# Second layer: small VectorE work and four inputs between product and sum, and the last image's output in one piece

## The chip, the cores and the metric

The kernel runs on one core of a Trainium2 chip. The metric is the device time of one execution in microseconds (us). Five engines work side by side, each through its own queue: PE (TensorE, matmuls), DVE (VectorE), ACT (ScalarE), POOL (GpSimd) and SP (SyncE, which here only issues DMA transfers). All data are 32-bit floats.

## The reference

Sixteen images of 128 channels and 56x56 pixels go through two layers. The first is a block of windowed attention with a two-layer perceptron; the change doesn't touch it. The second, cut to what matters:

```python
y = conv3x3(x, conv_w) + conv_b
seq = y.reshape(B * H * W, 8, 16)            # 8 tokens of 16 channels
xi, z = split(seq @ in_proj)
xc = silu(causal_conv(xi) + conv1d_b)
dt, Bm, Cm = split(xc @ x_proj)
dt = softplus(dt * dt_proj_w + dt_proj_b)
dA, dBx = exp(dt * A), dt * Bm * xc
for l in range(8):
    h = dA[l] * h + dBx[l]                   # 32 x 16 state values of each sequence
    ym[l] = sum(h * Cm[l]) + D * xc[l]
out = (ym * silu(z)) @ out_proj
return x + silu(group_norm(out) * gn_w + gn_b)
```

The recurrence over the eight tokens, `h = a*h + b`, is the heart of it: a product with the decay and a sum with the input.

## The kernel before

`layer0` runs first and leaves its result in DRAM, one tensor `x1[b]` of 128 x 3136 for each image. `layer1` reads it and does the second layer. It begins at about 3200 us of the span.

**Groups and steps.** An image is cut into seven groups of 448 sequences, so there are 112 groups. The outer loop runs over groups (`i`), the inner over 14 steps (`k`, 0 to 13). A state tile `h` of one token has 128 partitions (16 states and 8 of the 32 inner channels) by four quarters of 448 columns. One step handles one token and one half of the quarters (`jp`), 128x896 elements. The loop is software-pipelined: in step `k` the state of step `k` is advanced, while the decays are prepared two steps ahead, the inputs are taken in four steps ahead and spread on PE five steps ahead. Ahead of group `i`'s own steps, pieces for groups `i+1`, `i+2` and of the past groups are done by `work(i, k)`, which returns three lists, for PE and ACT, for DVE and for POOL.

**What stands in a step**, in the order in which it is issued before:

- `advance`: on DVE the product `a = a*h(l-1)` (line 947, in PSUM) and at once the sum `h(l) = a + h(l)` (948), which reads it. Steps 12 and 13 are the last token, which has no input: only a product (945), straight into `h`.
- `inject` (937, DVE): the input of a later token, `h = x*bb`. `x` is one PSUM buffer that PE fills, and `bb` is a row broadcast from DRAM.
- `decay` (919, PE): the exponents of the step two ahead, into one of two PSUM buffers `a`.
- `spread` (930, PE): fills `x` for the input of the next step, so it must wait until `inject` has read `x`.
- `decay_exp` (922, ACT): the exponential of `a`, in place.
- `weigh` (952, POOL, odd steps): `cst = h*cb`, 128x1792.
- the lists of `work`, DVE's first, then PE's, then POOL's.

The order of each engine's queue is that of the program, fixed by `_chain`.

**What `work` adds to DVE.** Step 0: `direct_mul` (906), twice 128x448, on a PSUM result that `direct` (901, PE) makes in step 13 of the group before. Steps 3 and 12: `collect` (974), 128x448. Steps 9 and 10 after a group with an odd number, and step 9 after the last group of an image: `statistics` (1022, with one 1024 for each image). So in four groups of seven there is at least one statistic.

**What `work` adds elsewhere, so far as it matters here.** PE: in step 12 `inner` for the group two ahead (838, 839), in step 13 `direct`, `skip` (967) and a `gather` (961), in step 0 two gathers, in step 1 a gather and `rate` (851), in step 3 `gate` (877), in step 4 `inner` again, in steps 5 and 6 `project_out` (995), in steps 5 to 9 the convolution of the next image (788), in step 11 `sequences` (830). ACT: `rate_log` (862, 863) in steps 5 and 7. POOL: `rate_sum` (868 to 871) in steps 6 and 8, `product` (897) in step 10.

**Buffers.** `h` and `cst` have four buffers, `x` one, `a` two. An input takes the `h` buffer of four tokens before, when `weigh` has read it: the input issued in step 12 takes that of the `weigh` of step 9.

**The end of an image.** Statistics, `group_mean`, `deviation`, `group_var` and `affine` run one to three groups later. Then `normalise` (1062, ACT) applies Silu in eight pieces of 392 columns, each between a load of the Silu table and one of the table for exponentials, `residual` (1053 to 1058) loads the image's `x1` in two halves into a single buffer `res`, and `store` (1067 on POOL, 1070 to 1072 on SP) adds and writes the whole image at the end. For the last image these groups hold nothing else: the loop runs seven groups beyond the last.

Of the kernel before, what the change touches and what calls it, by code (L numbers as in the profile page):

```python
# [10 lines left out]
F32 = mybir.dt.float32  # L11
U32 = mybir.dt.uint32
AF = mybir.ActivationFunctionType
# [4 lines left out]
P = 128  # L18
H = W = 56
HW = H * W  # L20
# [4 lines left out]
NBLK = HW // BLK  # L25
# [119 lines left out]
def _act_set(tc, name):  # L145
    tc.keep_in_program_order(tc.nc.scalar.preload_act_table_set(name))  # L146
# [566 lines left out]
def layer1(ctx: ExitStack, tc: tile.TileContext, x1, t, out):  # L713
# [99 lines left out]
    def own(jp):  # L813
        return slice(2 * jp, 2 * jp + 2)
# [124 lines left out]
    def advance(p, l, jp):  # L939

        a, before = p["a", l, jp], p["h", l - 1][:, own(jp), :]
        if l == 7:
            if jp == 0:
                p["h", l] = w4.tile([P, 4, BLK], F32, tag="h", name=f"h_{p['n']}_{l}")
            nc.vector.tensor_mul(p["h", l][:, own(jp), :], a, before)
        else:
            nc.vector.tensor_mul(a, a, before)  # L947
            nc.vector.tensor_add(p["h", l][:, own(jp), :], a, p["h", l][:, own(jp), :])  # L948

    def weigh(p, l):  # L950
        c = p["c", l] = w4.tile([P, 4, BLK], F32, tag="cst", name=f"cst_{p['n']}_{l}")
# [95 lines left out]
        nc.gpsimd.tensor_sub(gst[:, 5:6], gn_b, gst[:, 5:6])  # L1047

    half = HW // 2

    def residual(b, k):
        res = norms[b, k] = w1.tile([P, half], F32, tag="res", name=f"res_{b}_{k}")
        nc.sync.dma_start(res[0:64], x1[b][0:64, k * half : (k + 1) * half])
        if k == 0:
            nc.sync.dma_start(res[64:P], x1[b][64:P, 64 : half + 64])
        else:
            nc.sync.dma_start(res[64:P, 0 : half - 64], x1[b][64:P, half + 64 : HW])
            nc.sync.dma_start(res[64:P, half - 64 : half], x1[b][64:P, 0:64])
# [5 lines left out]
    def store(b, k, q):  # L1064
        part = slice(q * half // 2, (q + 1) * half // 2)
        xr = xrs[b][:, k * half : (k + 1) * half][:, part]
        nc.gpsimd.tensor_add(xr, xr, norms[b, k][:, part])
        if k == q == 1:
            xr = xrs[b]
            nc.sync.dma_start(outv[b, 0], xr[0:64])  # L1070
            nc.sync.dma_start(outv[b, 1, :, 64:HW], xr[64:P, 0 : HW - 64])
            nc.sync.dma_start(outv[b, 1, :, 0:64], xr[64:P, HW - 64 : HW])

    def work(i, k):


        def at(n):
            return groups[n] if 0 <= n < len(groups) else None  # L1080

        p, nxt, far, prev = at(i), at(i + 1), at(i + 2), at(i - 1)
        pe, dve, pool = [], [], []

        if prev:
            if k == 0:
                pe += [partial(gather, prev, 5), partial(gather, prev, 6)]
            if k == 1:
                pe.append(partial(gather, prev, 7))
            if k == 3:  # L1090
                dve.append(partial(collect, prev, 1))
            if k == 4:
                pool.append(partial(gated, prev, 1))
            if k in (5, 6):
                pe.append(partial(project_out, prev, k - 5))
            b = prev["b"]
            if prev["g"] % 2 and k in (9, 10):
                dve.append(partial(statistics, b, prev["g"] - 10 + k))
            if prev["g"] == NBLK - 1:
                if k == 9:  # L1100
                    dve.append(partial(statistics, b, NBLK - 1))
                if k == 12:
                    residual(b, 0)
        two = at(i - 2)
        if two and two["g"] == NBLK - 1:
            b = two["b"]
            if k == 3:
                pool.append(partial(deviation, b))
        three = at(i - 3)
        if three and three["g"] == NBLK - 1:  # L1110
            if k == 1:
                pe.insert(0, partial(group_var, three["b"], 0))
            if k == 2:
                pool.append(partial(affine, three["b"]))

        eighth = []
        for n in range(3, 7):
            past = at(i - n)
            if past and past["g"] == NBLK - 1 and k in (4, 12):
                eighth.append(partial(normalise, past["b"], 2 * (n - 3) + k // 12))  # L1120
        for n in range(4, 8):
            past = at(i - n)
            if past and past["g"] == NBLK - 1 and k == 2:
                pool.append(partial(store, past["b"], (n - 4) // 2, n % 2))
                if n == 5:
                    pool.append(partial(residual, past["b"], 1))

        if p:
            if k == 0:
                dve.append(partial(direct_mul, p))  # L1130
            if k == 7:
                pe.append(partial(skip, p, 0))
            if k in (8, 9, 10):
                pe.append(partial(gather, p, k - 7))
            if k == 12:
                dve.append(partial(collect, p, 0))
            if k == 13:
                if nxt:
                    pe.append(partial(direct, nxt))
                pe += [partial(skip, p, 1), partial(gather, p, 4)]  # L1140
                pool.append(partial(gated, p, 0))
            if k in (2, 6):
                bring(p, 0, {2: (4, 5), 6: (6,)}[k])
            if k in (1, 5, 9):
                bring(p, 1, {1: (3, 4), 5: (5, 6), 9: (7,)}[k])

        if nxt:
            if k in (1, 2):
                pe.append(partial(rate, nxt, k - 1))
            if k in (2, 6):  # L1150
                pe.append(partial(rate_exp, nxt, k // 4))
            if k in (5, 7):
                pe.append(partial(rate_log, nxt, k // 2 - 2))
            if k in (6, 8):
                pool.append(partial(rate_sum, nxt, k // 2 - 3))
            if k == 3:
                pe += [partial(gate, nxt, 0), partial(gate, nxt, 1)]
            if k == 4:
                eighth.insert(0, partial(inner, nxt, "zs", wz, w2, 0.0))
            if k == 7:  # L1160
                bring(nxt, 0, (0, 1))
            if k == 8:
                bring(nxt, 1, (1, 2))
            if k == 11:
                bring(nxt, 0, (2, 3))
            if k == 10:
                pool.append(partial(product, nxt))
            if k == 13 and not p:
                pe.append(partial(direct, nxt))

        if p and k in (5, 6, 7, 8, 9) and p["b"] + 1 < NB:
            taps = {5: (0, 1), 6: (2, 3), 7: (4,), 8: (5, 6), 9: (7, 8)}[k]
            pe.append(partial(convolve, p["b"] + 1, p["g"], taps))
        if p and p["g"] == NBLK - 1 and k == 11 and p["b"] + 2 < NB:
            load_image(p["b"] + 2)
        if two and two["g"] == NBLK - 1 and k == 2:
            pe.append(partial(group_mean, two["b"], 0))
        if far:
            if k == 11:
                pe.append(partial(sequences, far))  # L1180
            if k == 12:
                eighth.insert(0, partial(inner, far, "xc", wx, w3, c1_b))
        if eighth:
            pe = eighth + [partial(_act_set, tc, EXP_LN)] + pe
        return pe, dve, pool

    def state_step(i, k):

        i, k = i + k // 14, k % 14
        return (groups[i], 1 + k // 2, k % 2) if i < len(groups) else None  # L1190

    def input_step(i, k):
        i, k = i + k // 14, k % 14
        return (groups[i], k // 2, k % 2) if i < len(groups) else None
# [4 lines left out]
        convolve(0, i, range(9))  # L1199
    if NB > 1:  # L1200
        load_image(1)
    for i in range(-2, len(groups) + 7):
        for k in range(14):
            now = 0 <= i < len(groups)
            if now:
                advance(*state_step(i, k))
            inputs = input_step(i, k + 4) if now or (i == -1 and k >= 10) else None
            if inputs:
                inject(*inputs)
            decays = state_step(i, k + 2) if now or (i == -1 and k >= 12) else None  # L1210
            if decays:
                decay(*decays)
            inputs = input_step(i, k + 5) if now or (i == -1 and k >= 9) else None
            if inputs:
                spread(*inputs)
            if decays:
                decay_exp(*decays)
            if now and k % 2:
                weigh(groups[i], 1 + k // 2)
            pe, dve, pool = work(i, k)  # L1220
            for part in (dve, pe, pool):
                for step in part:
                    step()
    _chain(tc, start)


# [34 lines left out]
```

## Time and profile before

| | |
|---|---|
| device time, median of three runs | 8380.8 us (8372.44 to 8384.7) |
| profiled execution: span, and its own time | 8384.7 us, 8386.68 us |
| PE busy in the span | 7889.6 us, 94% |
| DVE | 7747.0 us, 92% |
| POOL | 7036.3 us, 84% |
| ACT | 5662.9 us, 68% |
| DMA of the main queue, share of 16 engines | 34.7% |
| mean granted TensorE clock | 0.983 |

The span runs from the first to the last instruction of one profiled execution. Busy time of PE is modelled at the end of each matmul. In the chain of work that ended last, DVE holds 40% of the span, POOL 24%, PE 18%, ACT 7%, and 11% is time in which an engine waited for nothing that the profile shows. The second layer's three DVE groups of 128x896, lines 937, 947 and 948, hold 11%, 10% and 6% of it by line.

The end of the span: the last product of the recurrence starts at 8333.14 us, the last statistics at 8344.24, the first Silu of the last image at 8348.72, the last output is issued from 8374.55 to 8378.4, and the span ends at 8384.7.

### The profile page before, as it was taken

The numbers are of one execution on the slowest core, as the hardware profiler recorded it, in microseconds if no ns is written. First come the engines' busy times: TensorE is split into PE (matmuls) and PEld (weight loads), VectorE is DVE, ScalarE is ACT, GpSimd is POOL, SyncE is SP. The second block draws the span as 40 slices with busy tenths as digits, with TensorE's granted clock in tenths as the row PEclk, the third lists the DMA queues.
The fourth block names the chain that finished last, engine by engine and source line by source line (L and its number), as shares of the span: only waits on it lengthen the run. The fifth ranks groups of instructions, "written<-read, shape, count | busy, mean of one in ns | idle before, by whom it ended". The sixth has DMA issues, their size and how long they took to land.

```text
span 8384.7 us, 151590 instructions
## 1 busy us (share of the span) xinstructions
PE 7889.6 (94%) x52860; PEld 3323.8 (40%) x52860; DVE 7747.0 (92%) x10358; ACT 5662.9 (68%) x10598; POOL 7036.3 (84%) x5664
## 2 busy tenths in 40 slices
PE   6999999999999987999999999999999999999997
PEld 2444444444444443333333333333333333333332
DVE  7999999999999874999999999999999999999997
ACT  4777767777777654666666666666666666666665
POOL 5888888888887724899999999999999989999987
PEclk8999999999999998999999999999999999999998
DMA  2333333333333222334334334334334333343333
GB/s 60 86 86 87 86 89 87 87 87 87 87 88 88 75 74 70 85 92 105 92 94 107 86 96 108 83 103 108 83 103 103 87 101 102 88 104 102 88 90 81
DMA packets 764424, 757.86 MB, mean 90 GB/s; under 512 B 188688, under 2 KB 663952, under 8 KB 761616
## 3 DMA queue, kind: packets, MB, share of 16 engines
q1 hardware_dynamic: 763664, 748.18, 34.7%
q8 instruction: 422, 6.91, 0.4%
q14 instruction: 338, 2.77, 0.1%
HBM read 439.61 MB, written 102.76 MB: 65 GB/s over the span
## 4 chain that ended last, share of the span: by engine, by line
DVE 40%; POOL 24%; PE 18%; issue 11%; ACT 7%; DMA 1%; SPq 0%; POOLq 0%; ACTq 0%; DVEq 0%
DVE h L937 11%; DVE a L947 10%; DVE h L948 6%; POOL cst L952 5%; POOL xh L264 4%; POOL e L380 4%; DVE lepe L461 4%; PE a L919 4%; POOL tap L262 3%; PE x L930 2%; POOL dtx L871 2%; PE pq L788 2%; DVE sst L364 2%; PE pq L961 2%; DVE ud L906 2%
## 5 line engine op out<-in xcount | busy, mean ns | idle before, releaser
L952 POOL TENSOR_TENSOR cst<-h,cb 128x1792 f32<-128x1792 f32 x784 | 3129.4, 3998 | 374.8 <-DVE h L948 301.2
L922 ACT ACTIVATE a<-a 128x896 f32<-128x896 f32 x1568 | 1416.4, 903 | 1119.0 <-PE x L930 681.5
L937 DVE TENSOR_TENSOR h<-x,bb 128x896 f32<-128x896 f32 x1568 | 1697.7, 1083 | 164.0 <-PE x L930 123.7
L461 DVE SCALAR_TENSOR_TENSOR lepe<-vpad,lep,lepe 128x448 f32<-128x448 f32 x2688 | 1718.7, 679 | 0.6
L930 PE MATMUL x<-dtx,amask 32*128 32x448 f32 x6272 | 1618.5, 592 | 32.5 <-DVE h L937 24.9
L919 PE MATMUL a<-dt,adec 32*128 32x448 f32 x6272 | 1615.6, 591 | 35.4 <-DVE h L948 15.9
L948 DVE TENSOR_TENSOR h<-a,h 128x896 f32<-128x896 f32 x1344 | 1467.0, 1092 | 45.8
L947 DVE TENSOR_TENSOR a<-a,h 128x896 f32<-128x896 f32 x1344 | 1465.5, 1090 | 6.0 <-ACT a L922 6.0
L380 POOL TENSOR_SCALAR e<-e,sst,zero 128x256 f32<-128x256 f32 x1568 | 861.3, 559 | 454.9 <-DVE sst L376 390.7
L370 ACT ACTIVATE e<-ps,sst 128x256 f32<-128x256 f32 x1568 | 729.6, 470 | 543.0 <-DVE sst L364 488.1
L788 PE MATMUL pq<-x1pad,conv 128*128 128x448 f32 x2016 | 886.5, 559 | 27.5 <-DMA x1pad<-x 19.2
L919 PEld LDWEIGHTS a<-dt,adec 32*128 32x128 f32 x6272 | 472.4, 184 | 1050.7 <-DVE h L948 469.1
L264 POOL TENSOR_TENSOR xh<-xh,tap 128x448 f32<-128x448 f32 x735 | 841.8, 1145 | 42.6
L961 PE MATMUL pq<-cst,sel 128*32 128x448 f32 x6272 | 730.4, 551 | 1.0 <-POOL cst L952 1.0
L146 ACT ACT_TABLE_LOAD x491 | 630.0, 1283 | 9.5 <-PEq L1252 0.7
L402 PE MATMUL ptt<-ident,e 128*128 128x128 f32 x3136 | 545.6, 285 | 92.3 <-POOL e L380 74.5
L930 PEld LDWEIGHTS x<-dtx,amask 32*128 32x128 f32 x6272 | 473.3, 184 | 398.8 <-DVE h L937 378.2
L364 DVE TENSOR_REDUCE sst<-ps 128x2 f32<-128x512 f32 x784 | 540.6, 690 | 88.7 <-PE ps L358 67.1
L358 PE MATMUL ps<-sel,q 32*64 32x256 f32 x6272 | 540.2, 413 | 70.9 <-ACT e L370 64.0
L262 POOL TENSOR_SCALAR tap<-xpad,pos,zero 128x448 f32<-128x448 f32 x735 | 532.3, 724 | 34.4
L402 PEld LDWEIGHTS ptt<-ident,e 128*128 128x128 f32 x3136 | 367.0, 142 | 417.7 <-POOL e L380 240.7
L788 PEld LDWEIGHTS pq<-x1pad,conv 128*128 128x128 f32 x2016 | 348.6, 190 | 412.9 <-issue 392.6
(163 smaller groups left out, 12116.2 us busy)
## 6 DMA issues: line engine op xcount, KB each, us to landing
sel<-kv SPq DMA_DIRECT2D x3136, 64.0 KB
bb<-db SPq DMA_DIRECT2D x336, 448.0 KB
cb<-dc SPq DMA_DIRECT2D x336, 448.0 KB
xpad<-x SPq DMA_DIRECT2D x32, 784.0 KB
x<-r SPq DMA_DIRECT2D x112, 224.0 KB
x1pad<-x SPq DMA_DIRECT2D x16, 1568.0 KB
db<-bs SPq DMA_DIRECT2D x112, 224.0 KB
dc<-cs SPq DMA_DIRECT2D x112, 224.0 KB
```

Source lines behind the costliest of these rows:

```text
L264: nc.gpsimd.tensor_add(im["xh"][i], im["xh"][i], held["tap"])
L380: nc.gpsimd.tensor_scalar(e, e, im["st", w][:, 2, p : p + 1], zero, ALU.mult, ALU.add)
L402: nc.tensor.transpose(ptt[:, P * (2 * p + h) : P * (2 * p + h + 1)], e[:, h * P : (h + 1) * P], ident)
L461: nc.vector.scalar_tensor_tensor(out, src, lep[:, k : k + 1], acc, ALU.mult, ALU.add)
L788: nc.tensor.matmul(pc, lhsT=conv[:, k, :], rhs=pad[:, 8 * i + dy : 8 * i + dy + 8, dx : dx + W], start=(k == 0), stop=(k == 8),)
L919: nc.tensor.matmul(a[:, k, :], lhsT=adec[rows, l4, :], rhs=p["dt"][rows, h, :], start=True, stop=True)
L922: nc.scalar.activation(p["a", l, jp], p["a", l, jp], AF.Exp)
L930: nc.tensor.matmul(x[:, k, :], lhsT=mask[rows, l4, :], rhs=p["dtx"][rows, h, :], start=True, stop=True)
L937: nc.vector.tensor_mul(p["h", l][:, own(jp), :], px["x"], weight)
L947: nc.vector.tensor_mul(a, a, before)
L948: nc.vector.tensor_add(p["h", l][:, own(jp), :], a, p["h", l][:, own(jp), :])
L952: nc.gpsimd.tensor_mul(c, p["h", l], p["gate", 1, l].unsqueeze(1).to_broadcast([P, 4, BLK]))
```

## The change

Three things are changed, all in `layer1`.

1. `advance` keeps the product alone; the sum moves to a new function `complete`. Between the two the loop now runs DVE's list from `work` (`direct_mul`, `collect`, `statistics`).
2. In steps 2, 7, 10 and 11 (`BETWEEN`), where that list is empty, `inject` stands between product and sum instead, and `spread` for the next step is issued ahead of `decay` on PE. In the other steps the order is product, list, sum, input.
3. For the last image `finish` takes the place of `normalise` and `store`: one load of the Silu table, then four times Silu on ACT and an add on DVE, and the output in two halves. Its two residual halves are loaded in steps 4 and 6 of the last group, the second into a buffer of its own (that of an image's `xr`). The loop ends four groups earlier.

```diff
@@ advance
             nc.vector.tensor_mul(p["h", l][:, own(jp), :], a, before)
         else:
             nc.vector.tensor_mul(a, a, before)
-            nc.vector.tensor_add(p["h", l][:, own(jp), :], a, p["h", l][:, own(jp), :])
+
+    def complete(p, l, jp):
+        if l < 7:
+            h = p["h", l][:, own(jp), :]
+            nc.vector.tensor_add(h, p["a", l, jp], h)
@@ residual
+    BETWEEN = (2, 7, 10, 11)
     def residual(b, k):
-        res = norms[b, k] = w1.tile([P, half], F32, tag="res", name=f"res_{b}_{k}")
+        pool, tag = (w2, "xr") if b == NB - 1 and k == 1 else (w1, "res")
+        res = norms[b, k] = pool.tile([P, half], F32, tag=tag, name=f"res_{b}_{k}")
@@
+    def finish(b):
+        gst = norms[b][2]
+        _act_set(tc, SILU)
+        for k in range(2):
+            out, res = xrs[b][:, k * half : (k + 1) * half], norms[b, k]
+            for q in range(2):
+                part = slice(q * half // 2, (q + 1) * half // 2)
+                nc.scalar.activation(out[:, part], out[:, part], AF.Silu, bias=gst[:, 5:6], scale=gst[:, 4:5])
+                nc.vector.tensor_add(res[:, part], res[:, part], out[:, part])
+            at = k * half
+            nc.sync.dma_start(outv[b, 0, :, at : at + half], res[0:64])
+            if k == 0:
+                nc.sync.dma_start(outv[b, 1, :, 64 : half + 64], res[64:P])
+            else:
+                nc.sync.dma_start(outv[b, 1, :, half + 64 : HW], res[64:P, 0 : half - 64])
+                nc.sync.dma_start(outv[b, 1, :, 0:64], res[64:P, half - 64 : half])
@@ work
-                if k == 12:
+                if k == 12 and b < NB - 1:
                     residual(b, 0)
...
                 pool.append(partial(affine, three["b"]))
+                if three["b"] == NB - 1:
+                    pool.append(partial(finish, three["b"]))
...
         if p:
+            if i == len(groups) - 1 and k in (4, 6):
+                residual(p["b"], k // 2 - 2)
@@ the loop
-    for i in range(-2, len(groups) + 7):
+    for i in range(-2, len(groups) + 3):
         for k in range(14):
             now = 0 <= i < len(groups)
+            pe, dve, pool = work(i, k)
+            inputs = input_step(i, k + 4) if now or (i == -1 and k >= 10) else None
+            further = input_step(i, k + 5) if now or (i == -1 and k >= 9) else None
+            decays = state_step(i, k + 2) if now or (i == -1 and k >= 12) else None
+
+            between = k in BETWEEN and not dve
             if now:
                 advance(*state_step(i, k))
-            inputs = input_step(i, k + 4) if now or (i == -1 and k >= 10) else None
+            for part in dve:
+                part()
+            if now and not between:
+                complete(*state_step(i, k))
             if inputs:
                 inject(*inputs)
-            decays = state_step(i, k + 2) if now or (i == -1 and k >= 12) else None
+            if now and between:
+                complete(*state_step(i, k))
+            if further and between:
+                spread(*further)
             if decays:
                 decay(*decays)
-            inputs = input_step(i, k + 5) if now or (i == -1 and k >= 9) else None
-            if inputs:
-                spread(*inputs)
+            if further and not between:
+                spread(*further)
             if decays:
                 decay_exp(*decays)
             if now and k % 2:
                 weigh(groups[i], 1 + k // 2)
-            pe, dve, pool = work(i, k)
-            for part in (dve, pe, pool):
-                for step in part:
-                    step()
+            for part in pe + pool:
+                part()
```

The computation is the same; `normalise` and `store` remain for the other images.

More of the change, by code (lines that the diff above doesn't have):

```diff
@@ L1118, in work @@
             past = at(i - n)
-            if past and past["g"] == NBLK - 1 and k in (4, 12):
+            if past and past["g"] == NBLK - 1 and past["b"] < NB - 1 and k in (4, 12):
                 eighth.append(partial(normalise, past["b"], 2 * (n - 3) + k // 12))
@@ L1122, in work @@
             past = at(i - n)
-            if past and past["g"] == NBLK - 1 and k == 2:
+            if past and past["g"] == NBLK - 1 and past["b"] < NB - 1 and k == 2:
                 pool.append(partial(store, past["b"], (n - 4) // 2, n % 2))
```

## The prediction

> **What bounds the kernel now.** The change touches the second layer alone, so I first cut the span into stretches and took one of a thousand microseconds out of the second layer (columns: span, then busy time of PE, weight load, DVE, ACT and POOL, clock, DMA share).
>
> ```profile
> 4600.00:5600.00 1000.00, 985.60 (x5147) 358.42 (x5145) 975.42 (x996) 676.30 (x949) 911.20 (x432) 1.00 0.37 96
> ```
>
> DVE is busy 97.5%, POOL 91%, and PE looks full but its ends are modelled. A group of 448 tokens takes 45.28 us (5025.77 to 5071.05 below). Next the groups of DVE instructions between 3300 and 8340 us: busy us and mean ns, then idle time and what ended it.
>
> ```profile
> L937 DVE TENSOR_TENSOR h<-x,bb 128x896 f32<-128x896 f32 x1553 | 1681.4, 1083 | 62.1 <-POOL cst L952 38.6 <-PE x L930 21.8 <-DMA bb<-db 0.8
> L948 DVE TENSOR_TENSOR h<-a,h 128x896 f32<-128x896 f32 x1332 | 1453.9, 1092 | 45.4
> L947 DVE TENSOR_TENSOR a<-a,h 128x896 f32<-128x896 f32 x1332 | 1452.4, 1090 | 5.8 <-ACT a L922 5.8
> ```
>
> DVE hardly ever waits for another engine; its largest wait is for POOL's L952. Then the timeline of one group's start (start us, us, engine, line):
>
> ```profile
> 5025.77 1.09 DVE L937 TENSOR_TENSOR h<-x,bb 128x896 f32<-128x896 f32 x1 [0.66 <-POOL cst L952]
> 5026.78 0.61 DVE L974 TENSOR_TENSOR ym<-pq,ud 128x448 f32<-128x448 f32 x1
> 5026.91 1.02 PE L930 MATMUL x<-dtx,amask 32*128 32x448 f32 x4 [0.48 <-DVE h L937]
> 5027.31 1.08 DVE L945 TENSOR_TENSOR h<-a,h 128x896 f32<-128x896 f32 x1
> 5027.86 1.77 PE L838 MATMUL pq<-seq,wx 128*128 128x448 f32 x4
> 5028.30 1.08 DVE L937 TENSOR_TENSOR h<-x,bb 128x896 f32<-128x896 f32 x1
> 5029.30 1.09 DVE L947 TENSOR_TENSOR a<-a,h 128x896 f32<-128x896 f32 x1
> 5029.56 0.65 PE L919 MATMUL a<-dt,adec 32*128 32x448 f32 x2
> 5030.43 1.09 DVE L948 TENSOR_TENSOR h<-a,h 128x896 f32<-128x896 f32 x1
> 5030.53 1.02 PE L901 MATMUL pq<-cs,cbm 128*128 128x448 f32 x2
> 5031.44 1.08 DVE L937 TENSOR_TENSOR h<-x,bb 128x896 f32<-128x896 f32 x1
> 5032.43 1.27 DVE L906 SCALAR_TENSOR_TENSOR ud<-pq,vec,dtx 128x448 f32<-128x448 f32 x2
> 5033.61 1.09 DVE L947 TENSOR_TENSOR a<-a,h 128x896 f32<-128x896 f32 x1
> ```
>
> Start to start, DVE goes on 1.00 us after an input (L937) and 1.01 after a sum (L948), but the sum starts 1.13 after the product it reads (5029.30, 5030.43). That 0.12 is what an instruction in between can fill. Second reading: L906 needs PE's L901 (5030.53 to 5031.55) and in this order meets it 0.9 us after it is done. And PE runs without a gap from 5026.91 on, released by the input of 5025.77: L930, L838, L919 with L930, L901.
>
> Last, the later part of the same group:
>
> ```profile
> 5052.95 1.10 DVE L947 TENSOR_TENSOR a<-a,h 128x896 f32<-128x896 f32 x1
> 5053.57 1.14 POOL L868 TENSOR_TENSOR u<-u,e 128x448 f32<-128x448 f32 x1 [0.47 <-ACT u L862]
> 5053.97 0.54 PE L930 MATMUL x<-dtx,amask 32*128 32x448 f32 x2
> ...
> 5067.02 3.99 POOL L952 TENSOR_TENSOR cst<-h,cb 128x1792 f32<-128x1792 f32 x1
> ...
> 5071.05 1.09 DVE L937 TENSOR_TENSOR h<-x,bb 128x896 f32<-128x896 f32 x1 [0.23 <-POOL cst L952]
> ```
>
> From 5053.57 POOL works back to back (four L868 to L871, L952, four more, L952) and ends at 5071.01; the input of step 12 needs the h buffer that this last L952 reads. So from step 5 on a group is as long as POOL's chain, and DVE has 0.2 us to spare where it also does two statistics, some 0.7 or more where it does none.
>
> [...] Here the dependent sum starts 0.12 us later than an independent instruction would; the measurement decides. [...] No run here shows DVE passing a waiting instruction. [...] L919 and L930, on different rows, take 0.97 us as a pair when both are ready (5029.56 to 5030.53), 1.02 each when not. A table load [...] shows 1.28 us here.
>
> **The change part by part.** I count steps 0 to 13 of a group. A group has 12 sums (steps 0 to 11). Separated are those of steps 0 (L906 twice), 3 (L974), 2, 7, 11 (the later input), 10 (input or statistics), and 9 in 4 of 7 groups: 6.6 of 12, at 0.12 worth 0.8 us a group, 88 us in 112 groups, if nothing waits. Now what waits. I cut the group at the input of step 12 and at the end of step 4's sum.
>
> First part, offsets from the input of step 12 (5025.77). Before: product of step 0 at 3.53, sum 4.66, input 5.67, L906 6.66, product of step 1 7.84, and so on to the end of step 4's sum, 5045.75, which is 19.98. After:
> - L974 of step 12 now stands ahead of this input. So product 13 starts at 1.01 and the input of step 13 could at 2.01; its L930 starts after the step-12 input ends and finishes at 2.16. PE to DVE takes 0.10 (L930 ends 5022.63, L937 starts 5022.73), so 2.26. Product of step 0: 3.26, 0.27 earlier than before.
> - L906 is reached at 4.26, but L901 ends at 5.78 (5031.55): PE's order is unchanged and hangs on the input of step 12. L906 starts at 5.88, a wait of 1.62 with the sum, the input and all later products queued behind it. Two L906 take 1.18: sum 7.06, input 8.07, product of step 1 9.07. That is 1.23 later than before.
> - Step 1 unchanged: sum 10.20, input 11.21, product of step 2 12.20. PE does L930 after the input that ends at 9.15 (9.20 to 10.15), then the gathers L961 (1.71, as at 5034.08), and is free at 11.85; L919 starts then, and L930 at 12.30 behind the input (12.29); as at 5023.87 it ends 1.05 later, 13.35. The input moved up in step 2 is reached at 13.20, starts at 13.45; sum 14.45, product of step 3 15.45: 0.12 won, 0.25 lost.
> - Step 3 wins its 0.12: L974 16.45, sum 16.98, input 17.99, product 18.98, sum 20.11, end 21.20. First part: +1.22.
>
> Second part, from that end: before 5071.01-5045.75, or 25.3, set by POOL. After, two paths. (a) PE does L919, L930 and the gates (L877, 1.72) after step 3's sum, which now has 0.53 less DVE work behind it, so the next L919 is 0.53 late, and ACT's exponential, table loads and L862 with it, and POOL's chain: 25.8. (b) DVE: the input moved up in step 7 wants to start at 5053.95, but its L930 ends at 5054.51: 5054.61, then sum 5055.61, product of step 8 5056.61 against 5056.09, 0.52 later. The statistics in steps 9 and 10 give 0.24 back, step 11's input loses 0.2 (its L930, behind the convolution, ends near 5067.9), L974 puts 0.53 ahead of step 12's input: 5071.56, 25.8. In groups without statistics step 10's input waits 0.6, but DVE had 0.7 spare; again 25.8. The two lie beside each other: +0.5, not +1.0.
>
> Sum: 21.2+25.8=47.0 against 45.28, +1.72 a group, 191 over 111 periods. Without the convolutions of the last seven groups and the sequence product of the last two, some 6 less.
>
> The end: before, eight Silu of 392 each stand between two table loads, and the one output issues at 8374.55. After, one load (8347.43 to 8348.71), four Silu of 784 (L1062's 0.71 for 392, and 0.32 more per 448 columns as L857 and L922 differ: about 1.0), the adds on DVE beside them (0.62 for 448, 1.09 for 896, so 0.97): last output at about 8353.7, 21 us earlier; what follows takes 10.2 before and hardly more after. Bounds: 15 to 24. In the last group the two residual loads go to SP ahead of some bb and cb loads (0.44+0.60+0.59 each); the second waits for the former image's output, issued by 8307.1, so a bb load may be late once: 0 to 3 us. I take 0.
>
> 191-6-21=+164. The profiled execution has a span of 8384.7 (8386.68 with what lies around it): 8549; from the median of the runs, 8380.8, 8545.
>
> **The rivals.**
> - Only L906 waits (all moved inputs find their data, second part unchanged): 1.22-0.25=0.97 a group, 108-21=+87: 8468. For it: PE's modelled ends could be late. Against: in step 7 it would have to be 0.6 us.
> - The waits add up, as path (a) delays step 7's product too and (b) comes on top: +1.22+0.5+0.5=2.2 a group, 246-27=+219: 8600. Against: the wait for L930 in step 7 covers the later product.
> - Faster: the products of PE are there in time. Then L974 fills the wait for POOL (0.53), steps 0, 2 and 3 win 0.36: 0.89 a group, 99+21=120: 8261. Place: L906 in step 0. With a wait w there the first part changes by w-0.40; with the second part kept even by POOL, faster needs w below about 0.6. The trace asks for 1.62; it would take L901 a microsecond earlier relative to the product, and nothing ahead of it on PE is removed. For it: DVE is the busiest engine and 0.12 is real.
> - Even: a w near 0.6, or the pair order doing other than I read.
>
> **How the numbers follow.** Forecast 0.77 (8500 to 8590), only L906 0.08, adding up 0.06, faster 0.07, even 0.02. What a measurement here can tell is about 0.2%. Slower 0.91, same 0.02, faster 0.07. The range 8460 to 8605 takes the two slower rivals in and leaves the faster one out.
>
> **What would show it.** L906 should show idle time of about 1.6 us in each group, ended by PE's L901; L937 more idle time ended by L930, in steps 2, 7 and 13; L948's gap behind the product gone in some half of the sums; the period 47.0; DVE's busy share near 94%; POOL's L952 still ending the wait of step 12 in some groups; the end after the last L1024 some 21 us shorter. I am wrong if L906 does not wait, or if the period is below 45.3.

## The result and the profile after

The changed kernel takes 8603.1 us (median of four runs) against 8376.8 for the kernel before: 1.027 times as long, 95% interval 1.0253 to 1.0288, or +226 us. The forecast was slower, +164, with a range of 8460 to 8605. The profiled execution of the changed kernel has a span of 8607.8 us, 223.1 more than before. In it the stretch from the first group's step 12 to the last group's step 13 is 248.6 us longer, what follows is 23.4 us shorter (28.2 against 51.6), and what precedes is 2.1 shorter.

The chain of work that ended last, by engine, from the page after:

```profile
PE 56%; DVE 17%; POOL 14%; issue 6%; ACT 5%; DMA 0%; SPq 0%; POOLq 0%; DVEq 0%; ACTq 0%
```

PE, 18% of that chain before, has changed places with DVE's 40%. Over the same thousand microseconds of the second layer (span; busy PE, weight load, DVE, ACT, POOL; clock; DMA share):

```profile
4600.00:5600.00 1000.00, 961.53 (x4893) 351.53 (x4889) 921.15 (x948) 643.44 (x900) 866.47 (x409) 0.98 0.35 92
```

Every engine is less busy than before, DVE by 54 us in 1000: the same work takes longer, with more waiting in it. In the changed kernel the sum is line 952 and POOL's product with `cb` line 956; 906, 919, 930 and 937 keep their numbers. DVE's groups from 3300 to 8560 us (busy us and mean ns, then idle time before them and what ended it):

```profile
L937 DVE TENSOR_TENSOR h<-x,bb 128x896 f32<-128x896 f32 x1550 | 1678.6, 1083 | 179.9 <-PE x L930 102.6 <-issue 27.1 <-PE a L919 20.7
L947 DVE TENSOR_TENSOR a<-a,h 128x896 f32<-128x896 f32 x1328 | 1447.0, 1090 | 30.6 <-ACT a L922 30.6
L952 DVE TENSOR_TENSOR h<-a,h 128x896 f32<-128x896 f32 x1328 | 1439.0, 1084 | 20.5
L906 DVE SCALAR_TENSOR_TENSOR ud<-pq,vec,dtx 128x448 f32<-128x448 f32 x222 | 141.6, 680 | 172.8 <-PE pq L901 172.8
```

The gap ahead of the sum has fallen from 45.4 to 20.5 us: what the change does between product and sum, it does. But L906 now waits for PE's L901 in each of its 111 groups, 1.56 us on average. Before, it waited once, as its line from 3300 to 8340 us shows:

```profile
L906 DVE SCALAR_TENSOR_TENSOR ud<-pq,vec,dtx 128x448 f32<-128x448 f32 x222 | 140.7, 676 | 0.6 <-PE pq L901 0.6
```

The wait of L937 for L930 has grown from 21.8 to 102.6. POOL's product, the largest wait of before with 38.6 us, ends only two waits after, 0.6 us in all. The start of a group, to be laid beside that of before (lines of ACT, POOL, SP and some of PE are left out):

```profile
5016.35 1.08 DVE L937 TENSOR_TENSOR h<-x,bb 128x896 f32<-128x896 f32 x1
5017.48 1.02 PE L930 MATMUL x<-dtx,amask 32*128 32x448 f32 x4
5018.43 1.77 PE L838 MATMUL pq<-seq,wx 128*128 128x448 f32 x4
5018.55 1.09 DVE L937 TENSOR_TENSOR h<-x,bb 128x896 f32<-128x896 f32 x1
5019.56 1.09 DVE L947 TENSOR_TENSOR a<-a,h 128x896 f32<-128x896 f32 x1
5021.10 1.02 PE L901 MATMUL pq<-cs,cbm 128*128 128x448 f32 x2
5022.15 1.28 DVE L906 SCALAR_TENSOR_TENSOR ud<-pq,vec,dtx 128x448 f32<-128x448 f32 x2 [1.51 <-PE pq L901]
5023.35 1.08 DVE L952 TENSOR_TENSOR h<-a,h 128x896 f32<-128x896 f32 x1
5024.35 1.08 DVE L937 TENSOR_TENSOR h<-x,bb 128x896 f32<-128x896 f32 x1
5024.48 1.02 PE L919 MATMUL a<-dt,adec 32*128 32x448 f32 x4 [0.72 <-DVE h L952]
5025.34 1.09 DVE L947 TENSOR_TENSOR a<-a,h 128x896 f32<-128x896 f32 x1
```

From the first line, PE's chain L930, L838, (L919 with L930), L901 is as long as before. DVE reaches L906 at 5020.6 and stands until L901 ends, at 5022.12; the sum, the input and the next product are queued behind it. The last line but one is new: PE, held by the late sum (the exponents go into the buffer `a` that this sum reads), stands idle for 0.72 us. Further on in the group:

```profile
5045.12 1.10 DVE L947 TENSOR_TENSOR a<-a,h 128x896 f32<-128x896 f32 x1 [0.38 <-ACT a L922]
...
5045.71 0.54 PE L930 MATMUL x<-dtx,amask 32*128 32x448 f32 x2
5045.73 1.14 POOL L868 TENSOR_TENSOR u<-u,e 128x448 f32<-128x448 f32 x1 [0.99 <-ACT u L862]
...
5046.34 1.09 DVE L937 TENSOR_TENSOR h<-x,bb 128x896 f32<-128x896 f32 x1
...
5059.89 1.09 DVE L937 TENSOR_TENSOR h<-x,bb 128x896 f32<-128x896 f32 x1 [0.29 <-PE x L930]
...
5062.89 0.61 DVE L978 TENSOR_TENSOR ym<-pq,ud 128x448 f32<-128x448 f32 x1
...
5063.43 1.08 DVE L937 TENSOR_TENSOR h<-x,bb 128x896 f32<-128x896 f32 x1
```

The input moved up in step 7 follows L930's end (5046.25) by 0.09; step 11's waits 0.29; step 12's no longer waits for POOL but for L978 in front of it. From 5016.35 to 5063.43 are 47.08 us; the forecast's sum was 47.0.

That is an undisturbed group. Of 111 periods 60 are 47.0 to 47.1 us and 14 more are 47.4, but 30 of the first 104 are 48.2 to 49.9. Three periods, with the clock in the last column but two:

```profile
5014.80:5061.90 47.10, 45.47 (x236) 16.84 (x234) 44.32 (x48) 30.86 (x44) 40.24 (x22) 1.00 0.29 79
5202.90:5251.30 48.40, 46.70 (x234) 16.76 (x232) 44.26 (x48) 30.72 (x43) 42.66 (x20) 0.96 0.44 117
4633.00:4682.80 49.80, 46.70 (x236) 16.45 (x234) 43.62 (x46) 29.91 (x42) 40.08 (x22) 0.93 0.27 74
```

All 30 long ones hold a stretch in which PE was granted half the clock, and none of the other 74 does. In the second of the three, on PE:

```profile
5212.57 1.02 PE L919 MATMUL a<-dt,adec 32*128 32x448 f32 x4 [0.72 <-DVE h L952]
5213.66 1.02 PE L930 MATMUL x<-dtx,amask 32*128 32x448 f32 x4
5214.61 2.89 PE L965 MATMUL pq<-cst,sel 128*32 128x448 f32 x16
```

After the idle 0.72 us the sixteen L965 take 2.89 us, against 1.71 for the same sixteen in the undisturbed group. The trace's clock records give half the clock from 5215.0 on for 3.41 us; the stretch before it, with the idle time in it, and this one (columns as above):

```profile
5211.60:5215.00 3.40, 2.60 (x16) 0.79 (x16) 3.37 (x4) 1.14 (x2) 2.74 (x2) 1.00 0.73 182
5215.00:5218.41 3.41, 3.41 (x24) 0.94 (x16) 2.65 (x3) 0.00 (x0) 2.63 (x1) 0.50 0.00 0
```

Between 3300 and 8240 us there are 37 such drops after, 133 us in all, and 11 before, 48 us. This is the largest part of what the forecast lacked.

### The profile page after: what moved, and what is told of

Read it like the earlier page. It is cut to its first block, busy times and chain, and to the rows that moved or that the text cites. A ratio compares the mean times of both kernels' runs of the same rounds, so it can differ in the third digit from the quotient of the medians.

```text
span 8607.8 us, 151798 instructions
## 1 busy us (share of the span) xinstructions
PE 8023.7 (93%) x52860; PEld 3386.1 (39%) x52860; DVE 7713.1 (90%) x10362; ACT 5638.8 (66%) x10579; POOL 7017.4 (82%) x5660
## 4 chain that ended last, share of the span: by engine, by line
PE 56%; DVE 17%; POOL 14%; issue 6%; ACT 5%; DMA 0%; SPq 0%; POOLq 0%; DVEq 0%; ACTq 0%
PE a L919 14%; PE x L930 10%; PE pq L788 10%; PE pq L965 5%; POOL xh L264 5%; POOL e L380 4%; PE pq L838 4%; DVE h L952 4%; DVE lepe L461 3%; DVE h L937 3%; POOL tap L262 3%; PE pq L999 2%; PE pq L877 2%; DVE sst L364 2%; DVE a L947 1%
## 5 line engine op out<-in xcount | busy, mean ns | idle before, releaser
L956 POOL TENSOR_TENSOR cst<-h,cb 128x1792 f32<-128x1792 f32 x784 | 3126.9, 3995 | 590.3 <-DVE h L952 357.9
L937 DVE TENSOR_TENSOR h<-x,bb 128x896 f32<-128x896 f32 x1568 | 1698.2, 1083 | 284.6 <-PE x L930 204.0
L919 PE MATMUL a<-dt,adec 32*128 32x448 f32 x6272 | 1638.4, 599 | 135.2 <-DVE h L952 134.7
L930 PE MATMUL x<-dtx,amask 32*128 32x448 f32 x6272 | 1637.7, 598 | 57.3 <-DVE h L937 41.1
L919 PEld LDWEIGHTS a<-dt,adec 32*128 32x128 f32 x6272 | 480.0, 187 | 1007.6 <-DVE h L952 533.1
L965 PE MATMUL pq<-cst,sel 128*32 128x448 f32 x6272 | 771.2, 579 | 0.3 <-POOL cst L956 0.3
L930 PEld LDWEIGHTS x<-dtx,amask 32*128 32x128 f32 x6272 | 485.3, 187 | 618.3 <-DVE h L937 393.0
```

The lines of the kernel that those rows point to most:

```text
L919: nc.tensor.matmul(a[:, k, :], lhsT=adec[rows, l4, :], rhs=p["dt"][rows, h, :], start=True, stop=True)
L930: nc.tensor.matmul(x[:, k, :], lhsT=mask[rows, l4, :], rhs=p["dtx"][rows, h, :], start=True, stop=True)
L937: nc.vector.tensor_mul(p["h", l][:, own(jp), :], px["x"], weight)
L956: nc.gpsimd.tensor_mul(c, p["h", l], p["gate", 1, l].unsqueeze(1).to_broadcast([P, 4, BLK]))
L965: nc.tensor.matmul(py[32 * j : 32 * j + 32], lhsT=sel[:, l4, :], rhs=p["c", l][:, j, :], start=False, stop=(l % 4 == 3), skip_group_check= ...
```

## The experiments

All kernels of this section have the change's new ending, so that each is to be read against `end_only`. Where the text says that work stands as before, DVE's list is issued behind the input, as in the kernel before. Each kernel was timed beside the kernel before (8373 to 8380 us in these runs).

| kernel | us, median | ratio to before, 95% interval | mean period, us | clock drops, 3300 to 8240 us |
|---|---|---|---|---|
| before | 8376.8 | 1 | 45.31 | 11 |
| changed | 8603.1 | 1.0270 (1.0253 to 1.0288) | 47.55 | 37 |
| end_only | 8360.0 | 0.9977 (0.9967 to 0.9986) | 45.32 | 7 |
| ud_only | 8511.6 | 1.0158 (1.0141 to 1.0175) | 46.59 | 28 |
| ud_back | 8414.8 | 1.0040 (1.0026 to 1.0055) | 45.86 | 16 |
| filled | 8572.7 | 1.0233 (1.0216 to 1.0250) | 47.15 | 4 |
| inputs_only | 8393.6 | 1.0016 (1.0009 to 1.0023) | 45.63 | 8 |
| ym3_only | 8391.7 | 1.0017 (1.0010 to 1.0023) | 45.59 | 18 |
| small_only | 8526.6 | 1.0173 (1.0156 to 1.0190) | 46.88 | 34 |
| stats_only | 8347.7 | 0.9970 (0.9958 to 0.9981) | 45.29 | 11 |
| pool_early | 8335.8 | 0.9948 (0.9931 to 0.9964) | 45.22 | 12 |
| pool_early_stats | 8316.3 | 0.9929 (0.9915 to 0.9942) | 44.97 | 8 |
| pool_early_small | 8350.4 | 0.9972 (0.9961 to 0.9983) | 45.27 | 8 |

The periods are the mean of 111 between the step-12 products of one profiled execution of each kernel. A clock drop is a stretch of half clock in its clock records. Since the mean clock differs from run to run (0.975 to 0.978 in the four of the changed kernel), the text also gives what a change does to a group at full clock: of the first 104 periods, those without any half clock, compared place by place in the image, as its seven groups differ by up to 0.9 us (in the kernel before 44.8 to 45.7). By this measure `end_only` and the kernel before agree within 0.01 us a group.

**The ending alone.**

```diff
-    BETWEEN = (2, 7, 10, 11)
+    BETWEEN = ()
+    EARLY = ()
             if now:
                 advance(*state_step(i, k))
-            for part in dve:
-                part()
+            if k in EARLY:
+                for part in dve:
+                    part()
...
+            if k not in EARLY:
+                for part in dve:
+                    part()
             for part in pe + pool:
                 part()
```

`EARLY` names the steps in which DVE's list stands between product and sum.

> The kernel before with the last image's new ending alone: in every step product, sum, input and the small work stand as before. By the prediction's sum the ending is worth 21 us (15 to 24): about 8356 against 8377. Rival: what follows the last output is bound by DMA, so that issuing earlier gains little, under 8 us.

It is 20 us faster than before, and the periods are those of before. The ending in the changed kernel:

```profile
8595.20 3.84 ACT L1088 ACTIVATE xr<-xr,gst 128x784 f32<-128x784 f32 x4
8596.27 3.77 DVE L1089 TENSOR_TENSOR res<-res,xr 128x784 f32<-128x784 f32 x4 [5.21 <-ACT xr L1088]
```

Four Silu of 0.96 and four adds of 0.94 us lie beside each other where eight Silu stood between table loads before. The gain is real and of the size that was summed; the loss is all in the rest.

**L906 alone between product and sum.** The same with `EARLY = (0,)`.

> New ending, and of the moves only L906 (the two products of the group's direct part) between product and sum in step 0. Theory (DVE stands still behind L906 until PE's L901 is done, 1.3 us a group with everything behind it late by 1.2): 137 us more than with the new ending alone, about 8493, and up to 8550 if PE's idle time in step 0 also lowers its clock. Rival (the moved inputs, not L906, make the loss): within 20 us of the new ending alone.

8511.6, 152 us more than the ending alone, where 137 were expected, and up to 8550 in all if the clock falls too: the theory, and more than three fifths of the whole loss, from one instruction pair in one step. At full clock a group is 1.15 us longer, 1.13 to 1.19 in each of the seven places of an image. Who DVE waited for, in this kernel and then in `end_only` (us in total, times, longest):

```profile
DVE ud L906 <- PE pq L901: 135.1, 108, 3.9
```

```profile
DVE ud L906 <- PE pq L901: 0.6, 1, 0.6
```

**L906 put back, all else as changed.** `EARLY = (3, 9, 10, 12)`, `BETWEEN = (2, 7, 10, 11)`.

> The changed kernel with L906 alone put back behind the input of step 0. Theory: the first part of a group is 0.2 us shorter than before, the second 0.5 longer, so about 45.5 us a group and 8386 in all, with PE's clock as steady as before. Rival (the moved inputs make the loss): above 8500.

8414.8: 188 us less than the changed kernel, 55 more than the ending alone where 26 were expected. In its profile 59 periods are 45.6 us and 17 are 45.5, near what was worked out; 13 are 47.0, the second groups of as many images, each with a clock drop, and 16 drops lie in the stretch against 7. At full clock a group is 0.42 us longer than with the ending alone, where 0.2 had been worked out. So the moved inputs and the other small work cost time, some 43 us in 104 groups, and clock drops the rest.

**PE kept busy during the wait.** A matmul of zeros is added to the sum in PSUM, behind the last matmul of step 13.

```diff
+    zeros = cst.tile([P, P], F32, tag="zeros1", name="zeros1")
+    nc.vector.memset(zeros, 0.0)
...
-                pe += [partial(skip, p, 1), partial(gather, p, 4)]
+                pe += [partial(skip, p, 1), partial(gather, p, 4), partial(busy, p)]
...
+    def busy(p):
+        nc.tensor.matmul(
+            pq[1][:, 0:320], lhsT=zeros, rhs=p["xc"][:, 1, 0:320], start=False, stop=False, skip_group_check=True
+        )
```

> The changed kernel with one more matmul on PE in step 13, zeros times xc over 320 columns added to the sum in PSUM, so that PE is busy while DVE waits in step 0; all waits of DVE stay. Theory for what the prediction left out (62 us): PE's idle 0.8 us in step 0 lowers its granted clock for 3.4 us in every third group; with it filled the periods of 48.2 to 49.9 us go back to 47.0 and the time falls by 40 to 60 us, to about 8550. Rival (the long periods come from DMA or from ACT's table loads): unchanged within 10 us, or longer by the added matmul.

8572.7, 30 us less than the changed kernel (its profiled execution 46 less), though PE has more to do. 83 of the periods are now 47.0 or 47.1, four drops are left of 37, and the sum of the periods falls by 44.3 us. PE's idle time ended by the sum, in the kernel before, in the changed kernel and here, where lines 919 and 952 have become 921 and 954:

```profile
PE a L919 <- DVE h L948: 8.5, 21, 1.4
```

```profile
PE a L919 <- DVE h L952: 123.1, 196, 0.7
```

```profile
PE a L921 <- DVE h L954: 47.0, 91, 0.6
```

L906 waits as long as in the changed kernel (161.2 us by 8300, against 164.0), and a group at full clock is as long to 0.03 us. So the idle time of PE, and not DMA or ACT's tables, made the long periods. The median fell somewhat less than the 40 expected at least: of the four runs of each kernel the profiled one is the slowest of the changed kernel and the fastest here, so that the 44 us of the profiles are more than a usual pair of runs would show.

**The moved inputs alone.** `EARLY = ()`, `BETWEEN = (2, 7, 10, 11)`.

> New ending and, of the moves, only the later input between product and sum in steps 2, 7, 10 and 11; the small work stands as before. Theory: step 2 costs 0.13 us a group (its input waits 0.26 for PE's L930 and saves 0.12), steps 7 to 11 nothing, since POOL's chain sets that part: 45.4 us a group, about 8375, and more only where PE's clock drops. Rival (the 0.12 comes free wherever something stands between): 0.5 us a group less, about 8305.

8393.6: 34 us more than the ending alone, where 15 were expected and the rival said 55 less. Who ended DVE's waits:

```profile
DVE h L937 <- PE x L930: 78.7, 217, 0.6
...
DVE h L937 <- POOL cst L956: 2.1, 3, 1.1
```

In `end_only` these are 19.1 and 37.5 us. The wait for POOL is gone, replaced by a larger one for PE: in steps 7 to 11 the moved inputs use up all that DVE had to spare there and a little more, which the theory had put at nothing. By 8240 us, 56.7 us of it stand ahead of step 7's input and 21.0 ahead of step 2's. The clock has no part in the loss: at full clock a group is 0.34 us longer (36 us in 104 groups). The groups that take 44.8 us in `end_only` become 45.5 to 45.7, those of 45.6 to 45.8 lose some 0.1.

**L974 of step 3 alone.** `EARLY = (3,)`.

> New ending and, of the moves, only L974 of step 3 between product and sum. Theory: DVE wins 0.12, but step 4's sum now comes 0.5 us sooner behind step 3's, PE has its L919, L930 and the gates to do between the two, so ACT's and POOL's chain starts 0.5 late; in the four groups of seven with Silu pieces, which POOL sets, 0.4 us longer, in the others 0.1 shorter: about 8380. Rival (one small instruction between brings its 0.12 everywhere): 13 us less than the new ending alone, about 8347.

8391.7, 32 more than the ending alone. The rival is out by its sign. DVE's waits for POOL's L956 rise from 37.5 to 55.0 us and those of the product for ACT from 4.6 to 23.7, which is the shift of ACT's chain. But at full clock a group is only 0.12 us longer, 12 of the 26 us by which the first 104 periods grew; the rest lies in periods with half clock (18 drops against 7; the mean granted clock is 0.977 to 0.982 in its 20 runs, against 0.983 to 0.985 in the ten of `end_only`).

**All small work, no moved input.** `EARLY = (0, 3, 9, 10, 12)`, `BETWEEN = ()`.

> The changed kernel without the moved inputs: all small work between product and sum, every input behind its sum. Theory: L906 still waits 1.6 us; periods of about 46.9 in groups that POOL sets and 46.4 in the others, 8515, and up to 40 us more if PE's clock drops. Rival (the moved inputs bring what they were counted for, 0.5 us a group): slower than the changed kernel, above 8640.

8526.6, in the expected band, and 76 less than the changed kernel. The moved inputs, counted alone, save gaps; with the rest they cost a third of the loss, 0.57 us a group at full clock (60 us in 104 groups) and clock drops on top. Against `ud_only` the small work other than L906 adds 15 us. L974 of step 12 was not moved by itself.

**Is it POOL that sets the second part?** Nothing of the change is in this kernel but the ending.

```diff
-            if k in (5, 7):
-                pe.append(partial(rate_log, nxt, k // 2 - 2))
-            if k in (6, 8):
-                pool.append(partial(rate_sum, nxt, k // 2 - 3))
+            if k == 7:
+                pe.append(partial(rate_log, nxt, 1))
+            if k in (4, 8):
+                pool.append(partial(rate_sum, nxt, k // 4 - 1))
             if k == 3:
-                pe += [partial(gate, nxt, 0), partial(gate, nxt, 1)]
+                pe += [partial(gate, nxt, 0), partial(gate, nxt, 1), partial(rate_log, nxt, 0)]
```

> New ending, small work and inputs as before, and one thing of neither kernel: rate_log of the first half moves from step 5 to the end of step 3 (ahead of the table loads) and its rate_sum on POOL from step 6 to step 4, where POOL stands idle. Theory (POOL's chain sets the second part of a group): POOL is done some 2 us earlier before step 12, the wait of L937 for L952 goes, and a group is 0.2 to 0.5 us shorter where POOL set it, 20 to 40 us in all: about 8330. Rival (DVE alone sets the period): within 8 us of the new ending alone.

8335.8, 24 us less than the ending alone. The wait of L937 for POOL is gone; what DVE waits for most is now ACT:

```profile
DVE a L947 <- ACT a L922: 32.2, 79, 1.3
DVE h L937 <- PE x L930: 26.0, 97, 1.8
```

At full clock a group is 0.17 us shorter, 18 us in 104 groups. Over all periods it is 11 us (45.22 against 45.32), since the profiled execution has 12 drops (75 us) against 7 (34 us); its first group comes 12 us earlier, no more than that start varies among profiles of kernels that are alike up to there (3284 to 3300 us). So POOL did set that part. The wait for ACT now stands ahead of step 7's product, where `end_only` waited 4.6 us; the move itself puts 1.2 us of ACT's work (L862, L863) ahead of the exponentials there, so whether ACT was next in line anyway is not shown.

**The statistics, with POOL as before and with POOL moved forward.** `EARLY = (9, 10)` on `end_only`, and on `pool_early`.

> New ending, and of the moves the statistics alone between product and sum, POOL's order as before. Theory (from step 5 to step 12 a group is as long as POOL's chain, so what DVE saves there becomes wait for L952): within 6 us of the new ending alone, about 8357, with more wait of L937 for L952. Rival: 13 us faster than the new ending alone, as with POOL moved forward.

> The kernel with POOL's rate_sum moved forward and the new ending, and of the moves the statistics alone, between product and sum in steps 9 and 10. Theory: the statistics wait for nothing and nothing is queued on their sum's lateness; now that POOL no longer sets that part, each of the seven in an image wins its 0.12, 13 us in all: about 8323 against 8336. Rival (PE, near its limit in steps 5 to 10, takes it back): within 5 us of 8336.

Against its own kernel before, `stats_only` wins 27 us, `end_only` 20: the 7 in between are less than the error of the two ratios, and between the two expectations. In its profile the wait for L956 rises from 37.5 to 45.2 us. With POOL forward the gain over `pool_early` is 13 of 13 expected (56 us under the kernel before, against 43), but these two ratios have overlapping intervals as well, so that the medians don't tell 7 from 13. The periods at full clock do: the statistics make a group 0.08 us shorter with POOL as before (8 us in 104 groups) and 0.14 with POOL forward (14 us). With POOL as before, the groups with two statistics win 0.28 and two of the three with none lose 0.23; with POOL forward, the former win 0.27 and these two lose nothing. This is the fastest version of the study, 0.9929 times the time before.

**And L974 on top of it.** `EARLY = (3, 9, 10)` on `pool_early`.

> As the kernel with the statistics between, and L974 of step 3 between product and sum as well. Theory: L974 wins 0.12 on DVE, but PE's gates still make the exponentials of step 6 and 7 half a microsecond late against DVE, and with POOL out of the way it is step 7's product that waits for ACT; in the groups with Silu pieces 0.3 longer, in the others 0.1 shorter: 5 to 20 us slower than without it. Rival (POOL's chain was the only price of L974's place): 13 us faster than without it.

34 us slower than without it, more than the 20 expected. The one wait that changes:

```profile
DVE a L947 <- ACT a L922: 74.5, 113, 1.3
```

It was 29.6 us without L974 there. The small instruction saves its 0.12 and brings 0.4 us of waiting for ACT a group; at full clock a group is 0.28 longer, so here the clock has hardly a part.

## Why the prediction was right, and where it was short

**The number.** Slower was right, and so was most of the mechanism. But 8603.1 lies above the 8500 to 8590 that the forecast itself stood for, and only 2 us inside the range, whose upper edge was set for the rival in which the waits add up, and that is not what happened. That the range holds the result is in part luck.

**First part of the group.** Right, nearly to the tenth. With the input of step 12 at 0 (5016.35), the prediction has the input of step 13 at 2.26, L906 at 5.88, product 1 at 9.07, product 3 at 15.45, step 4's sum at 20.11; the profile has 2.20, 5.80, 8.99, 15.40 and 20.05. Step 2's input waits 0.18 and not 0.25, since the L930 taken as its model lasts 1.02 us and not 1.05. That L906 carries this part is shown by `ud_only` and `ud_back`.

**Second part.** Predicted 25.8, found 25.9 in this group. Both paths were seen: POOL's last product ends at 5063.18, DVE comes to the input at 5063.43. That they lie beside each other and don't add held, too. But DVE's path is the later one: that POOL would still end the wait of step 12 in some groups, one of the signs named, came in only two waits. DVE's busy share, another sign, is 94% in this group, as said, and 92% over the thousand us with their drops.

**PE's later input in steps 2, 7 and 11.** Right in kind; alone they cost 34 us (`inputs_only`), about twice the 15 expected of that run.

**The ending.** 21 predicted, 23.4 in the profile, 20 in `end_only`. The late bb load in the last group, taken as 0 with a bound of 3, came: L937 waits 2.2 us there for its DMA.

**What was left out.** "1.72 a group, 191 over 111 periods" is 185 with its deductions; the profile has 248. Of the 63 us that are missing, some 42 are half clock: the sum has each PE time at full clock, and the term for what PE's idle time does to its clock isn't in it. The first 104 periods are 235 us longer than before, but 193 by the groups at full clock; with PE kept busy (`filled`), 44 us go. Some 14 are the groups at full clock themselves, 1.86 us longer and not 1.72, most of it in the first group of each image (47.36 against 44.98); the prediction worked out one group in the middle of an image and took it for all. The last 7 lie in the last image's seven groups (+13.0 instead of the +6 that the deduction gave), whose last one runs at half the clock for 37 of its 51 us (25 of 46 before). The prediction had PE's next matmuls start late behind the sum and the input of step 0, gave all that follows its usual duration, and didn't ask what the gap does by itself.

A drop lasts 3.41 us in 35 of the 37 and 6.83 in the other two. The 3.41 us ahead of 28 of them are 77% busy by the modelled ends, with no single gap above 0.73 us. The drops of this trace start on a grid of 3.413 us, to 0.01 us from 3310 to 8210. Of the stretches of this grid that are 77% busy 28 of 69 were followed by a drop, of those that are 62% busy 7 of 14, so no threshold can be given from these runs.

**The rivals.** Only L906: `ud_only` shows it to be 152 of the 243 us between `end_only` and the changed kernel, not all. The faster case needed L906's wait below 0.6 us; it is 1.56. Adding up would have given 8600, near the measured time, but for a reason that is not found: quiet groups are 47.0, not 47.5.

## What to carry to other kernels

The gap between a product and the sum that reads it is worth what it measures, here 0.12 us, and DVE, which in both traces went through every group from 3300 to 8240 us in the program's order, pays for filling it with the whole wait of what is put there, here 1.56 us a group for L906: look up when the filler's own operand is ready in the place it moves to, not in the place it comes from. Count a wait on one engine through to the next engine's idle time, and there ask for the clock: here PE waited 123.1 us for the sum and had 37 clock drops, and with the zeros of `filled` 47.0 us and 4. And a saving in a stretch that another engine sets was had in full here only once that engine had been moved out of the way: at full clock the statistics gave 0.08 us a group before POOL was moved, and 0.14 after.

## What the runs showed that had not been expected

- PE's granted clock halved for 3.41 us after 28 of 69 stretches of 3.41 us with only 0.8 us of idle time in them, none of it longer than 0.73 at once, and one drop costs a group 1.3 us (48.3 against 47.1), two 2.8. A matmul of zeros in the gap, 0.8 us of extra work by the modelled ends, made the kernel 30 us faster.
- Moving 0.53 us of DVE work (L974) from behind step 3's input to between its product and sum made ACT's exponentials late: 32 us lost where a gain of 13 would be counted, 12 of them by the groups at full clock, the rest where the clock is halved.
